# The row maxima of two cross-attentions, scheduled 1.4 units ahead of their scores instead of 2

## The chip, the core and the metric

The kernel runs on one core of a Trainium2 chip. The metric is the device time of one execution in microseconds (us). Engines: PE is TensorE (matrix products; PEld is its weight load), DVE is VectorE, ACT is ScalarE, POOL is GpSimd, SP is SyncE, which here only issues DMAs.

## The reference

A decoder of four layers works on `x`, 8 sequences of 256 tokens and 128 features, with a context of 1601 tokens and 64 features. Each layer adds a cross-attention to the context and then a feed-forward block. Attentions 0 and 3, which the change touches, have 16 heads of 8 features. Cut to what matters, for attention 0:

```
qh = (q @ Wq + bq).reshape(B, LQ, HEADS, D_K).transpose(0, 2, 1, 3)
kh = (k @ Wk + bk).reshape(B, LKV, HEADS, D_K).transpose(0, 2, 1, 3)
vh = (v @ Wv + bv).reshape(B, LKV, HEADS, D_K).transpose(0, 2, 1, 3)
scores = jnp.einsum('bhqd,bhkd->bhqk', qh, kh) * scale
attn = jax.nn.softmax(scores, axis=-1)
out = jnp.einsum('bhqk,bhkd->bhqd', attn, vh)
return concat @ Wo + bo
...
x = x + _L0_xattn_ref(_layernorm(x, axis=-1), ctx_512, ctx_512, ...)
```

The softmax needs, for each query and head, a number near the largest score, so that the exponential stays in range. Computing these maxima is the work that is moved here.

## The kernel before, in words

The function `narrow` does attention 0 at the start of the kernel and attention 3 near its end, each for the 8 sequences. The work of a sequence `b` is cut into four units of four heads, so an attention has 32 units, `n = 4 b + i`.

For a unit, `place` (lines 783 to 794) spreads keys and queries over the partitions with DMAs: 8 for the keys (on SP's queue) and 10 for the queries (on POOL's), into one of four places of a ring `K[n % 4]`, `Q[n % 4]`. A row of `Q`, zero at first, later holds minus the maximum, so that the score matmul itself subtracts it. Each place has two halves, `t` = 0 and 1, and each half holds two heads, one in partitions 0 to 63 and one in 64 to 127. Two matmuls on the two partition halves (`g` = 0, 1) can run side by side in the array.

Three pieces of work belong to a unit:

- *Maxima* (`maxima`, lines 796 to 823): 14 pairs and a shift. A pair is two matmuls into two buffers of the PSUM pool `pm` (line 807) and two DVE reduces (line 810) that take their row maxima. Twelve of the pairs have 512 columns in a matmul; the other two take the 66 columns left over, with four small matmuls each. `pm` has three buffers. The shift (lines 816 to 819) is three small DVE instructions that join the maxima and split them into two summands in `M`.
- *Placing the shift* (`place_shift`, lines 825 to 832): PE transposes `M` (line 828), ACT copies the result (line 830), and SP issues two DMAs that write the rows into `Q` (line 832).
- *Scores and values*: a unit has 7 steps `p` of two half steps `t`. A half step computes the scores of two chunks of 128 context tokens (`score`: line 994 on PE into buffers of pool `st`, of which there are four; line 997, two exponentials on ACT), then one chunk of values of the step before (`values`, line 1006 on PE). The first half step of a unit has the last chunk of the unit before, the second has none.

The order on each engine is the order in which the program writes the instructions; no scheduler changes it. In each half step of unit `n` the loop at the end of `narrow` writes: the scores, a chunk of values, then what is in the list `beside` and has come due (placing keys and queries for unit `n + 3`, placing the shift, projections of queries, keys and values for the next sequence, loads), then the maxima that are due. Each entry of `beside` has a share of the unit at which it is due.

The maxima of unit `n + 2` are spread over the 14 half steps of unit `n`. Unit 0 has two sets, those of units 1 and 2, and units 30 and 31 have none; unit 0's own maxima are done ahead of the loop. The shift of unit `n + 1` is placed at share 0.1 of unit `n`, which is half step 1; in unit 0 it is placed at the end.

In the last six units of attention 0 (from `AFTER = 26`), steps of the following feed-forward block for the first sequence stand in `beside` too.

The code that the diff touches, with the profile's line numbers:

Of the kernel before, what the change touches and what calls it, by code (L numbers as in the profile page):

```python
# [49 lines left out]
TAKEN = -3.0e38  # L50
KW = LK + 1
RING = 4
AFTER = 26


@with_exitstack
def decoder_kernel(ctx: ExitStack, tc: tile.TileContext, a: dict, out: bass.AP):
# [93 lines left out]
    for b in range(NB):  # L151
        x = const.tile([P, QT, D], F32, tag=f"x{b}", name=f"x{b}")
# [470 lines left out]
    def narrow(wq, wkT, wvT, wo, bq, bk, bv, bo, first, after=None):  # L623
# [8 lines left out]
        with ExitStack() as es:  # L632
# [163 lines left out]
            def maxima(n):  # L796

                mx = two.tile([P, QT, 4, 4], F32, tag="mx", name="mx", bufs=3)
                last = KW - 1536

                def pair(t, js, at, w):
                    k, q = K[n % RING][t], Q[n % RING][t]
                    pt = [pm() for g in range(2)]
                    for x, j in enumerate(js):
                        for g in range(2):
                            r = slice(64 * g, 64 * g + 64)
                            nc.tensor.matmul(pt[g][:, x * w:(x + 1) * w], lhsT=q[r, j * P:(j + 1) * P],  # L807
                                             rhs=k[r, at:at + w], start=True, stop=True)
                    for g in range(2):
                        nc.vector.tensor_reduce(mx[:, js[0]:js[-1] + 1, 2 * t + g, at // 512],  # L810
                                                pt[g][:, 0:len(js) * w].rearrange("p (j k) -> p j k", k=w),
                                                AX.X, ALU.max)

                def shift():
                    m = two.tile([P, QT, 4], F32, tag="mxn", name="mxn")
                    nc.vector.tensor_reduce(m, mx, AX.X, ALU.max, negate=True)
                    mq = M[n % 2].rearrange("p j (h s) -> p j h s", s=8)
                    nc.vector.tensor_copy(mq[:, :, :, 0], m)
                    nc.vector.tensor_tensor(mq[:, :, :, 1], m, mq[:, :, :, 0].bitcast(F32), ALU.subtract)

                return [f for t in range(2) for f in
                        (*(lambda j=j, t=t, at=at: pair(t, (j,), at, 512) for j in range(QT) for at in (0, 512, 1024)),
                         lambda t=t: pair(t, range(QT), 1536, last))], shift

            def place_shift(n):
                pt = bank()
                for j in range(QT):
                    nc.tensor.transpose(pt[0:32, j * P:(j + 1) * P], M[n % 2][:, j, :].bitcast(F32), ident)
                st = two.tile([32, LQ], F32, tag="st32", name="st32")
                nc.scalar.copy(st, pt[0:32, 0:LQ])  # L830
                for t in range(2):
                    nc.sync.dma_start(out=Q[n % RING][t][4:P:8, :].bitcast(F32), in_=st[16 * t:16 * t + 16, :])

# [100 lines left out]

            before = []
            steps = (NC + 1) // 2
            more = maxima(1)
            for n in range(units):
                b, i = divmod(n, 4)
                v = V[b % 2]  # L940

                ms = []
                if n == 0:
                    ms += [*more[0], more[1]]
                if n + 2 < units:
                    pairs, shift = maxima(n + 2)
                    ms += [*pairs, shift]
                due = [len(ms) * (x + 1) // (2 * steps) for x in range(2 * steps)]
                done = 0

                beside = []
                if n + 3 < units:
                    beside += [((0.0, 0.25)[t], lambda t=t: place(n + 3, t)) for t in range(2)]
                beside.append((0.3, lambda: load_later(3)))
                if n + 1 < units:
                    beside.append((1.0 if n == 0 else 0.1, lambda: place_shift(n + 1)))
                if b + 1 < NB and i == 0:
                    beside += zip((0.0, 0.2, 0.5, 0.65, 0.8, 1.0),
                                  (lambda: turn_y(b + 1), lambda: make_q(b + 1), *make_k(b + 1)))
                if b + 1 < NB and i == 1:  # L960
                    beside += zip((0.2, 0.4, 0.6, 0.8), make_v(b + 1))
                if b and i == 2:
                    beside += zip((0.2, 0.35, 0.6), finish(b - 1))
                if b + 2 < NB and i == 2:
                    load_ct(b + 2)
                    if first:
                        cuts, turns = make_ct(b + 2)
                        beside += zip((0.0, 0.0, 0.4, 0.6), cuts)
                        beside += zip((0.3, 0.5, 0.7, 0.9), turns)
                if b + 3 < NB and i == 3:  # L970
                    beside.append((0.0, lambda: load_raw(b + 3)))
                if b + 2 < NB and i == 3:
                    beside.append((0.5, lambda: (make_y(b + 2), add_bias(b + 2))))
                if after is not None and n >= AFTER:
                    if n == AFTER:
                        late = after(Scratch(), bank)
                    per = 2 * steps
                    beside += [((x - per * (n - AFTER)) / per, lambda x=x: run([late[x]], EARLY + LATE))
                               for x in late if x // per == n - AFTER]
                beside.sort(key=lambda x: x[0])  # L980
                if i == 0:
                    od[b] = two.tile([P, LQ], F32, tag="od", name="od")
                    sums[b] = two.tile([P, LQ], F32, tag="sums", name="sums")
                cell = {}

                def score(p, t, e):
                    k, q = K[n % RING][t], Q[n % RING][t]
                    cs = range(2 * p, min(2 * p + 2, NC))
                    m = P if cs[-1] < NC - 1 else LAST
                    st = [bank().rearrange("p (j q) -> p j q", q=LQ) for g in range(2)]  # L990
                    for j, c in enumerate(cs):
                        for g in range(2):
                            r = slice(64 * g, 64 * g + 64)
                            nc.tensor.matmul(st[g][0:m, j, :], lhsT=k[r, c * P:c * P + m], rhs=q[r, :],  # L994
                                             start=True, stop=True)
                    for g in range(2):
                        nc.scalar.activation(e[0:m, 2 * t + g, 0:len(cs), :], st[g][0:m, 0:len(cs), :], AF.Exp)  # L997

                def values(c, e, cell=cell, i=i, v=v, b=b):
                    if c == 0:  # L1000
                        cell["o"] = ps["o"].tile([P, LQ], F32, tag="o", name="ov")
                    m = P if c < NC - 1 else LAST
                    for g in range(4):
                        h = 4 * i + g
                        at = 2 * D * c + 32 * (h // 2) + 2 * (h % 2)
                        nc.tensor.matmul(cell["o"][32 * g:32 * g + 32, :], lhsT=v[0:m, at:at + 32],  # L1006
                                         rhs=e[0:m, g, c % 2, :], start=(c == 0), stop=(c == NC - 1))
                    if c == NC - 1:
                        os = two.tile([P, LQ], F32, tag="os", name="os")
                        nc.scalar.copy(os, cell["o"])  # L1010
                        at = slice(32 * i, 32 * i + 32)
                        nc.sync.dma_start(out=od[b][at, :], in_=os[0:P:4, :])
                        nc.sync.dma_start(out=sums[b][at, :], in_=os[1:P:4, :])

                for p in range(steps):
                    e = two.tile([P, 4, 2, LQ], F32, tag="e", name="e")
                    for t in range(2):
                        score(p, t, e)
                        if before:
                            before.pop(0)()  # L1020
                        while beside and (beside[0][0] * 2 * steps < 2 * p + t + 1 or p * t == steps - 1):
                            beside.pop(0)[1]()
                        for f in ms[done:due[2 * p + t]]:
                            f()
                        done = due[2 * p + t]
                    before = [lambda c=c, e=e, values=values: values(c, e)
                              for c in range(2 * p, min(2 * p + 2, NC))]
            for f in before + finish(NB - 1):
# [726 lines left out]
```

## Time and profile before

| what | value |
|---|---|
| median of 3 runs | 3657.8 us (3653.39 to 3658.94) |
| profiled execution, its own time | 3657.44 us |
| its span on the core | 3655.7 us |
| mean granted clock of TensorE | 0.968 |
| attention 0, first exponential to last copy of values | 65.8 to 743.9 us |
| attention 3, likewise | 2766.7 to 3418.2 us |

Times in the profile count from the start of the span. "Busy" is the time in which an engine works on at least one instruction; PE's matmuls overlap, and their ends are modelled, so a start is more certain than an end. A group of instructions gives the line, the engine, the tile written and those read, the size and the number; behind the bar stand busy time, the mean of one in ns, the idle time just before, and what ended it. In the timeline, equal instructions in a row are merged ("x4"), and idle time in brackets is followed by what ended it. In a table of stretches, a line is the stretch, its length, the busy time of PE, PEld, DVE, ACT and POOL with the number of instructions, the granted clock of TensorE (1.00 is full), the busy share of the DMA engines and what they moved in GB/s.

### The profile page before, as it was taken

The numbers are of one execution on the slowest core, as the hardware profiler recorded it, in microseconds if no ns is written. First come the engines' busy times: TensorE is split into PE (matmuls) and PEld (weight loads), VectorE is DVE, ScalarE is ACT, GpSimd is POOL, SyncE is SP. The second block draws the span as 40 slices with busy tenths as digits, with TensorE's granted clock in tenths as the row PEclk, the third lists the DMA queues.
The fourth block names the chain that finished last, engine by engine and source line by source line (L and its number), as shares of the span: only waits on it lengthen the run. The fifth ranks groups of instructions, "written<-read, shape, count | busy, mean of one in ns | idle before, by whom it ended". The sixth has DMA issues, their size and how long they took to land.

```text
span 3655.7 us, 74821 instructions
## 1 busy us (share of the span) xinstructions
PE 3437.5 (94%) x28363; PEld 2319.6 (63%) x28363; DVE 2600.6 (71%) x6564; ACT 2284.9 (63%) x5686; POOL 1126.8 (31%) x1993
## 2 busy tenths in 40 slices
PE   6999999979999999999999999988989999999799
PEld 3555555458777877787887878865434555555344
DVE  5788888656777766777777777675556888888365
ACT  2688888746566666666666666653223878888422
POOL 4344344614051513324150602020113333332100
PEclk9999999989999999999999999998985999999899
DMA  4354444230000001000000000020003444443100
GB/s 92 56 88 72 70 69 64 28 80 1 15 2 27 6 24 38 1 26 1 15 1 15 1 11 6 11 68 19 0 18 56 68 69 66 64 67 50 44 3 9
DMA packets 112118, 130.21 MB, mean 36 GB/s; under 512 B 67184, under 2 KB 95888, under 8 KB 111120
## 3 DMA queue, kind: packets, MB, share of 16 engines
q1 hardware_dynamic: 91024, 114.09, 18.3%
q0 software_dynamic: 20480, 10.53, 1.2%
q8 instruction: 225, 3.69, 0.4%
q10 hardware_dynamic: 256, 0.82, 0.2%
q14 instruction: 133, 1.09, 0.1%
HBM read 44.79 MB, written 11.28 MB: 15 GB/s over the span
## 4 chain that ended last, share of the span: by engine, by line
PE 79%; DVE 10%; ACT 6%; issue 2%; POOL 2%; DMA 1%; SPq 0%; ACTq 0%; DVEq 0%; POOLq 0%
PE ov L1006 13%; PE o L467 11%; PE st L420 11%; PE pm L807 10%; PE t L453 8%; PE st L994 6%; PE gu L1601 3%; PE gu L1602 3%; DVE mx L810 3%; PE o L1616 3%; ACT pt L455 2%; DVE ls L427 2%; PE st L778 2%; ACT e L441 1%; PE st L721 1%
## 5 line engine op out<-in xcount | busy, mean ns | idle before, releaser
L810 DVE TENSOR_REDUCE mx<-pm 128x1 f32<-128x512 f32 (+1 forms) x1792 | 1015.0, 626 | 221.6 <-PE pm L807 220.1
L997 ACT ACTIVATE e<-st 128x512 f32<-128x512 f32 (+1 forms) x1792 | 916.5, 564 | 250.0 <-PE st L994 193.2
L427 DVE TENSOR_REDUCE ls<-st 128x1 f32<-128x512 f32 x1088 | 548.7, 566 | 319.7 <-PE st L420 318.2
L441 ACT ACTIVATE e<-st,ls 128x512 f32<-128x512 f32 x1088 | 634.0, 602 | 12.8 <-DVE ls L430 12.0
L455 ACT COPY pt<-t 128x512 f32<-128x512 f32 x544 | 293.5, 586 | 460.4 <-PE t L453 459.7
L1006 PE MATMUL ov<-e,V 128*32 128x256 f32 x6656 | 556.1, 401 | 0.3 <-ACT e L997 0.3
L807 PE MATMUL pm<-K,Q 64*128 64x512 f32 (+1 forms) x2048 | 528.0, 468 | 26.9 <-DVE mx L810 19.4
L453 PE MATMUL t<-ident,e 128*128 128x128 f32 (+1 forms) x3536 | 507.1, 282 | 2.2
L467 PE MATMUL o<-pt,v 128*64 128x128 f32 (+1 forms) x7072 | 495.2, 280 | 11.9 <-DVE pt L455 7.9
L807 PEld LDWEIGHTS pm<-K,Q 64*128 64x128 f32 x2048 | 238.4, 195 | 374.6 <-DVE mx L810 261.2
L467 PEld LDWEIGHTS o<-pt,v 128*64 128x64 f32 (+1 forms) x7072 | 417.5, 139 | 83.0 <-issue 31.6
L453 PEld LDWEIGHTS t<-ident,e 128*128 128x128 f32 (+1 forms) x3536 | 392.4, 141 | 51.6 <-ACT pt L455 28.8
L994 PE MATMUL st<-Q,K 64*128 64x256 f32 (+1 forms) x3328 | 422.8, 296 | 0.3 <-ACT e L997 0.2
L420 PE MATMUL st<-ct,qh 128*128 128x512 f32 x1088 | 404.8, 372 | 2.3 <-ACT e L441 2.3
L994 PEld LDWEIGHTS st<-Q,K 64*128 64x128 f32 (+1 forms) x3328 | 343.8, 188 | 42.3 <-issue 14.6
L420 PE MATMUL st<-ct,ql 128*128 128x512 f32 x1088 | 361.8, 365 | 0.0
L793 POOL DMA_DIRECT2D Q<-qh x256 | 127.9, 500 | 469.3 <-PE st L994 415.9
L455 DVE COPY pt<-t 128x512 f32<-128x512 f32 (+1 forms) x544 | 239.1, 481 | 35.3 <-PE t L453 35.1
L420 PEld LDWEIGHTS st<-ct,qh 128*128 128x128 f32 x1088 | 204.7, 188 | 86.8 <-issue 38.4
L1604 ACT ACTIVATE act<-gu 128x512 f32<-128x512 f32 x132 | 78.8, 597 | 250.3 <-PE gu L1602 248.1
L441 ACT ACTIVATION_READ_ACCUMULATOR e<-st,ls 128x1 f32 x1088 | 230.7, 212 | 0.0
L420 PEld LDWEIGHTS st<-ct,ql 128*128 128x128 f32 x1088 | 205.5, 189 | 36.8
(444 smaller groups left out, 4205.5 us busy)
## 6 DMA issues: line engine op xcount, KB each, us to landing
K<-kh SPq DMA_DIRECT2D x252, 100.1 KB
K<-kl SPq DMA_DIRECT2D x252, 100.1 KB
ct<-ctd SPq DMA_DIRECT2D x24, 801.0 KB
ctd<-ct SPq DMA_DIRECT2D x8, 801.0 KB
v<-in_ctx SPq DMA_DIRECT2D x16, 384.0 KB
Q<-qh POOLq DMA_DIRECT2D x256, 16.0 KB, 2.5
Q<-ql POOLq DMA_DIRECT2D x256, 16.0 KB, 2.5
raw<-in_ctx SPq DMA_DIRECT2D x8, 384.0 KB
```

The source lines that it names most:

```text
L420: nc.tensor.matmul(st[n, c][:, 0:w], lhsT=q[k, h][i][:, j * P:(j + 1) * P], rhs=ct[k][:, at:at + w], start=(i == 0), stop=(i == 1))
L427: nc.vector.tensor_reduce(ls[n][:, c:c + 1], st[n, c][:, 0:BANK[c][1]], AX.X, ALU.max)
L441: nc.scalar.activation(e[n][:, at:at + w], st[n, c][:, 0:w], AF.Exp, bias=ls[n][:, 4:5], scale=1.0, accum_out=ls[n][:, 5 + c:6 + c])
L453: nc.tensor.transpose(t[0:m, (c - 4 * i) * P:(c - 4 * i + 1) * P], e[n][:, c * P:c * P + m], ident)
L455: (nc.scalar.copy if i < 2 else nc.vector.tensor_copy)(p[0:m, 0:w], t[0:m, 0:w])
L467: nc.tensor.matmul(o[n][half, 0:P], lhsT=v[k][0:m, c, :], rhs=turned[n, c // 4][0:m, (c % 4) * P:(c % 4 + 1) * P], start=(c < 2), stop=(c ...
L793: nc.gpsimd.dma_start(out=q[r:P:8, :].bitcast(F32), in_=qhl[b][r % 2][src, :].bitcast(F32))
L807: nc.tensor.matmul(pt[g][:, x * w:(x + 1) * w], lhsT=q[r, j * P:(j + 1) * P], rhs=k[r, at:at + w], start=True, stop=True)
L810: nc.vector.tensor_reduce(mx[:, js[0]:js[-1] + 1, 2 * t + g, at // 512], pt[g][:, 0:len(js) * w].rearrange("p (j k) -> p j k", k=w), AX.X, ...
L994: nc.tensor.matmul(st[g][0:m, j, :], lhsT=k[r, c * P:c * P + m], rhs=q[r, :], start=True, stop=True)
L997: nc.scalar.activation(e[0:m, 2 * t + g, 0:len(cs), :], st[g][0:m, 0:len(cs), :], AF.Exp)
L1006: nc.tensor.matmul(cell["o"][32 * g:32 * g + 32, :], lhsT=v[0:m, at:at + 32], rhs=e[0:m, g, c % 2, :], start=(c == 0), stop=(c == NC - 1))
```

## The change

The maxima are no longer tied to a unit's own list. A function `plan(m)` gives each of the 15 tasks of unit `m` (14 pairs, then the shift) a half step counted from the start of the attention, from half step 8 of unit `m - 2` up to half step 8 of unit `m - 1`, with the task's place rounded down; for unit 1 they start at 0. The loop then takes the tasks of each half step. The shift of unit `n + 1` is placed at share 9/14 of unit `n`. In the new kernel the lines behind the edit are three or four further down.

```diff
+DONE = 8
...
             steps = (NC + 1) // 2
-            more = maxima(1)
+            per = 2 * steps
+            tasks = {}
+
+            def plan(m):
+
+                pairs, shift = maxima(m)
+                first_, last_ = max(0, per * (m - 2) + DONE), per * (m - 1) + DONE
+                todo = [*pairs, shift]
+                for x, f in enumerate(todo):
+                    tasks.setdefault(first_ + (last_ - first_) * x // len(todo), []).append(f)
+
+            plan(1)
             for n in range(units):
                 b, i = divmod(n, 4)
                 v = V[b % 2]
-
-                ms = []
-                if n == 0:
-                    ms += [*more[0], more[1]]
                 if n + 2 < units:
-                    pairs, shift = maxima(n + 2)
-                    ms += [*pairs, shift]
-                due = [len(ms) * (x + 1) // (2 * steps) for x in range(2 * steps)]
-                done = 0
+                    plan(n + 2)
...
                 if n + 1 < units:
-                    beside.append((1.0 if n == 0 else 0.1, lambda: place_shift(n + 1)))
+                    beside.append(((DONE + 1) / per, lambda: place_shift(n + 1)))
...
-                        for f in ms[done:due[2 * p + t]]:
+                        for f in tasks.pop(per * n + 2 * p + t, []):
                             f()
-                        done = due[2 * p + t]
```

More of the change, by code (lines that the diff above doesn't have):

```diff
@@ L976, in narrow @@
                         late = after(Scratch(), bank)
-                    per = 2 * steps
                     beside += [((x - per * (n - AFTER)) / per, lambda x=x: run([late[x]], EARLY + LATE))
```

## The prediction

> **What bounds the kernel now.** I read the page first, then busy time in stretches cut at the units of the two attentions, then the PE timeline inside one unit, then the order of instructions of both kernels on each engine.
>
> ```profile
> PE 3437.5 (94%) x28363; PEld 2319.6 (63%) x28363; DVE 2600.6 (71%) x6564; ACT 2284.9 (63%) x5686; POOL 1126.8 (31%) x1993
> PE 79%; DVE 10%; ACT 6%; issue 2%; POOL 2%; DMA 1%; SPq 0%; ACTq 0%; DVEq 0%; POOLq 0%
> L810 DVE TENSOR_REDUCE mx<-pm 128x1 f32<-128x512 f32 (+1 forms) x1792 | 1015.0, 626 | 221.6 <-PE pm L807 220.1
> ```
>
> PE is busy 94% and is 79% of the chain. So I ask of each part of the change what it does to PE's own time, and where PE waits. By unit (attention 3: units 0, 1, 29, 30):
>
> ```profile
> 2764.70:2819.20 54.50, 49.83 (x227) 23.91 (x226) 31.78 (x58) 19.25 (x38) 11.32 (x19) 0.50 0.15 34
> 2819.20:2844.60 25.40, 25.40 (x218) 14.61 (x218) 16.36 (x32) 16.86 (x34) 4.01 (x9) 0.78 0.40 61
> 3368.30:3385.70 17.40, 17.40 (x193) 9.28 (x192) 16.30 (x32) 14.65 (x30) 0.00 (x0) 1.00 0.02 7
> 3385.70:3401.90 16.20, 15.98 (x168) 7.58 (x167) 3.50 (x9) 14.20 (x30) 0.91 (x2) 1.00 0.03 9
> ```
>
> [...]Unit 29 is filled by PE; DVE (16.3) and ACT (14.7) fit inside. Unit 30 has no maxima and is only 1.2 us shorter, since ACT then sets the pace. Unit 0 takes 54.5 us at a clock of 0.50. Attention 0's unit 0 is the same (54.5); its clock column reads 1.00, but its value matmuls last 633 ns, as at 0.50, against 403 ns later, so I go by durations.
>
> In cold unit 0 each half step has two pairs, four maxima matmuls on three pm buffers:
>
> ```profile
> 2780.25 1.22 PE L807 MATMUL pm<-K,Q 64*128 64x512 f32 x3
> 2781.83 0.79 PE L807 MATMUL pm<-K,Q 64*128 64x512 f32 x1 [0.36 <-DVE mx L810]
> 2781.83 1.21 PE L994 MATMUL st<-Q,K 64*128 64x256 f32 x4
> 2782.97 1.08 PE L1006 MATMUL ov<-e,V 128*32 128x256 f32 x8
> 2783.98 1.22 PE L807 MATMUL pm<-K,Q 64*128 64x512 f32 x3
> ```
>
> The fourth waits for the first's reduce: it starts 1.58 us after the first, and the scores behind it take 1.14 us to the values instead of 0.56, because the two row halves no longer run side by side. A half step is 3.73 us. A cold half step with one pair (unit 1) is 2.16.
>
> Warm, in unit 29:
>
> ```profile
> 3369.35 0.50 PE L807 MATMUL pm<-K,Q 64*128 64x512 f32 x2
> 3369.68 0.40 PE L994 MATMUL st<-Q,K 64*128 64x256 f32 x4
> 3370.01 0.39 PE L828 MATMUL st<-ident,M 128*32 128x128 f32 x2
> 3370.34 0.79 PE L807 MATMUL pm<-K,Q 64*128 64x512 f32 x2
> 3370.67 0.68 PE L994 MATMUL st<-Q,K 64*128 64x256 f32 x4
> 3371.28 0.64 PE L1006 MATMUL ov<-e,V 128*32 128x256 f32 x8
> 3371.85 0.51 PE L807 MATMUL pm<-K,Q 64*128 64x512 f32 x2
> ```
>
> A pair alone: maxima 0.33, scores 0.33, values 0.57, together 1.24 to 1.28 a half step. Half step 1 has no values, so its second maxima matmul comes early. It starts 0.29 after the first (0.79 where 0.50 is usual), which is 1.28 us after 3369.35: a pm buffer comes back only 1.28 us after it was taken (0.53 until the reduce starts, 0.69 reduce, 0.05 wake-up). That wait hides the transposes of line 828. The figure is 1.27 to 1.29 in nearly all undisturbed units.
>
> **Part 1: unit 0 loses seven pairs.** The order shows half steps 0 to 6 of unit 0 unchanged, half step 7 with the shift alone, 8 with two pairs, 9 to 13 with one. Seven pairs leave (28 before, 21 after); the other units keep 14, unit 30 gets the seven. Half steps 7 to 13 take 29.7 us in both attentions (starts of line 994). After, still cold: 7: 0.56 + 1.01 + 1.15 (K projection) = 2.72; 8: 0.56 + 1.01 + 1.57 = 3.14; 9: 1.14 + 1.01 + 0.26 (transposes) + 1.15 + 0.59 = 4.15; 10: 2.16; 11: 3.31; 12: 1.95; 13: 2.3. Sum 19.7, a gain of 10.0 each.
>
> Then the clock. It rises after a stretch of PE work without waits: in attention 3 from 2818.7 to 2830.9 (12 us), in attention 0 from 117.7 to at most 125.2 (6 to 7), at the end of attention 0 from 680.6 to 690 (9 to 10). I take 8. After, such a stretch starts at half step 9, with 13.9 us of cold work ahead in unit 0: 5.9 of it turns warm, saving 43% (1.24 against 2.16), 2.5 us. Unit 1's cold start goes too: 5.3 us of it in attention 0, 11.4 in attention 3, saving 2.3 and 4.9. Together (10.0 + 2.5) x 2 + 7.2 = 32 us. The Trainium skill ("TensorE: Matmul & The Clock Gate", Part 1 on the clock gate) says some 3.4 us of sustained work warm it; the rows show two to three times that. By the page the gain would be 36. I stay with the rows; 26 to 38 as bounds.
>
> **Part 2: every later unit gets a double step.** 15 tasks over 14 half steps, rounded down: tasks 0 and 1 both fall in half step 8, and the shift alone in 7. Before, each half step had exactly one pair, and the shift rode on the last. The order shows the four 512-column matmuls in a row once per unit, 29 warm units (1 to 29) in each attention. No such wait stands there before; nearest rows are the cold double step and the 1.28 us of half step 1, which agree. Half step 7 becomes 0.34 shorter. In 8, scores and values 0.90, then 1.28 to the fourth matmul (DVE has been idle, so nothing shortens it): 2.18 where 1.24 was. In 9, scores to values take 0.61 (3370.67 to 3371.28) where 0.33 was. Sum: -0.34 + 0.94 + 0.28 = +0.88. Behind the wait on PE stand scores, thus ACT's exponentials, but ACT has 2.7 us of slack per unit; PE has none to catch up with. Bounds 0 (all absorbed) and 1.2; I take 0.87.
>
> **Part 3: the shift rows move** from half step 1 to 9: two transposes (PE), one copy of 0.35 us (ACT), two DMA issues of 0.9 us (SP). At 1 the transposes lay under the 1.28 us wait, so taking them away frees nothing; at 9 the pm buffers have been freed (second reduce ends 1.82 us after the first matmul, needed at 2.5), so 0.32 us is bare (3370.01 to 3370.34). Bounds 0 and 0.35; I take 0.31. ACT's copy falls in slack. On SP the two issues now stand behind both halves of the next K placement and weight loads, all issued and nearly all moved 12 us into a unit; half step 9 is about there, and the rows are needed five half steps, over 6 us, later, against some 4 us for copy, issue and transfer. Cost nothing; if that cover went, 1 to 2 us a unit. The shift's own DVE work (0.7 us) moves from the unit's end to an idle spot, worth nothing where the 1.28 us rule already ruled. But in attention 0 the transposes at half step 1 do wait for it (0.27 us in six units; 0.75, 0.74 and 1.20 in units 26, 28, 30): about -4 us in all.
>
> **Part 4: unit 30.** Seven pairs more in an ACT-paced unit: half steps 0 to 6 go from 8.0 to 8.8 us (those of unit 29), +0.9 in attention 3; attention 0's share is in the -4. K placement, loads and POOL issues keep their places: 0, and K has more lead.
>
> **Sum.** 29 x 2 x (0.87 + 0.31) = +68.4; -32.2; +0.9; -4. Net +33 on the profiled execution's 3657.4 us, which is 0.4 below the median: 3691 us, 0.9% slower.
>
> **Rivals.** *Absorbed bunch (faster).* In steady state the second maxima matmul of many half steps starts 0.05 us after a reduce ends, so PE may really be paced by the buffer loop and could run ahead. Then half step 7 gives back what 8 costs, and only the transposes stay: 3657.4 - 35 + 18 = 3640 to 3645. It decides if the fourth matmul starts at most 0.57 us after the first. Against: it was 1.58 cold, the loop is 1.28, and reduces of 0.6 us cannot be shortened. 10%. *Half of it (no change):* a loss near 0.6 per unit balances the gain, 3657; 6%. *Clock stays cold in unit 0:* only the 20 us of part 1, 3703; 8%. *Clock falls at each double step.* In attention 0:
>
> ```profile
> 704.33 0.50 PE L994 MATMUL st<-Q,K 64*128 64x256 f32 x4
> 706.03 0.38 PE L828 MATMUL st<-ident,M 128*32 128x128 f32 x2 [1.20 <-DVE M L819]
> 706.33 0.50 PE L994 MATMUL st<-Q,K 64*128 64x256 f32 x4
> 706.77 0.64 PE L1006 MATMUL ov<-e,V 128*32 128x256 f32 x8
> 707.34 0.65 PE L994 MATMUL st<-Q,K 64*128 64x256 f32 x4
> 707.91 1.08 PE L1006 MATMUL ov<-e,V 128*32 128x256 f32 x8
> ```
>
> A wait of 1.20 us was followed by cold matmuls (1.08), one of 0.75 in unit 26 was not. Mine would show as 0.55: the third matmul starts 0.23 after the first and lasts 0.50, the fourth starts at 1.28. The same page (section on HAM oscillation) sets the danger at gaps over about 3.4 us; this trace puts it near 1, so the margin is 0.6 us and not 2.9. A fall costs 1.1 us (here) to 4.1 (after 680.6): over 58 units 3755 or more; 5%. That the change does not do what it says is excluded by the order of instructions.
>
> **How the numbers follow.** Main case 71%, 3691, own range 3672 to 3712: part 1 by 6 either way, part 2 and 3 by 0.2 a unit (12 us). Faster by over 0.2% 10%, within 0.2% (about what a measurement here can tell from no change) 6%, slower 84%. The range 3662 to 3718 takes in the colder clock and reaches toward the balance.
>
> **What would show it.** Right: unit 0 near 40 us with 403 ns values by its end; units 2 to 29 about 1.2 us longer; a row of three maxima matmuls, then one after a 0.5 us wait on line 810's reduce, at half step 8; waits of PE on DVE up by about 0.5 x 58. Wrong: units 2 to 29 as long as before (then it is faster), or 633 ns values inside them (then far slower).

## The result and the profile after

The changed kernel takes 3698.4 us (median of 4 runs, 3696.16 to 3702.51) beside 3655.6 before (4 runs, 3650.64 to 3658.94): a ratio of 1.0121 [1.0106, 1.0136], or 42.8 us slower. Its profiled execution took 3697.88 us, with a span of 3696.2 against 3655.7.

On the page, the work is the same and the path hardly changes its shape. The line of busy times, the chain by engine, and the group of the reduces:

```profile
PE 3437.7 (93%) x28363; PEld 2311.2 (63%) x28363; DVE 2595.2 (70%) x6564; ACT 2286.2 (62%) x5686; POOL 1125.8 (30%) x1993
PE 78%; DVE 11%; ACT 6%; issue 2%; POOL 2%; DMA 1%; SPq 1%; ACTq 0%; DVEq 0%; POOLq 0%
L811 DVE TENSOR_REDUCE mx<-pm 128x1 f32<-128x512 f32 (+1 forms) x1792 | 1011.9, 627 | 266.4 <-PE pm L808 265.0
```

PE's busy time is the same to 0.2 us (3437.5 before), although one part of the span became faster and another slower. What has grown is DVE's share of the chain (10% before) and its idle time ahead of the reduces (221.6 before). So the stages have to be read, and first the waits. Of each line of PE's waits, the columns are the total in us, how often, and the longest. Before:

```profile
PE pm L807 <- DVE mx L810: 19.4, 51, 2.3
```

After:

```profile
PE pm L808 <- DVE mx L811: 64.4, 160, 0.7
```

That is 45 us more waiting for a maxima buffer. 58 waits of 0.55 in the double half steps make 32 of it. In half step 1, where the transposes used to fill the buffer wait, 0.32 of it is now bare in every unit, 19 us in all; this costs no time (half step 1 of unit 29 takes 0.95 now and took 0.99 before). Unit 0 and unit 28 of attention 0 have some 6 us of waits less.

The stretches that answer to those of before are unit 0 (attention 0, then attention 3), and units 1, 29 and 30 of attention 3:

```profile
63.70:104.70 41.00, 38.24 (x211) 18.54 (x210) 23.83 (x43) 19.26 (x39) 14.04 (x19) 0.58 0.31 59
2779.40:2818.70 39.30, 36.71 (x211) 18.13 (x210) 23.76 (x43) 18.85 (x38) 9.64 (x15) 0.61 0.21 47
2818.70:2841.00 22.30, 21.44 (x219) 12.41 (x218) 16.18 (x32) 16.95 (x35) 5.34 (x12) 1.00 0.45 65
3404.50:3423.50 19.00, 18.12 (x194) 9.37 (x194) 16.32 (x32) 14.75 (x30) 0.00 (x0) 1.00 0.02 6
3423.50:3442.00 18.50, 17.69 (x184) 8.69 (x183) 11.09 (x23) 14.29 (x30) 0.91 (x2) 1.00 0.03 8
```

Unit 0 is 13 to 15 us shorter (54.5 before). Unit 1 runs at a clock of 1.00 instead of 0.78. But unit 29, which stands for units 1 to 29 of each attention, is 1.6 us longer with the same 16.3 us of DVE. PE's timeline in unit 29, half steps 7 to 9 (the columns are start and length), before:

```profile
3377.13 0.48 PE L994 MATMUL st<-Q,K 64*128 64x256 f32 x4
3377.54 0.64 PE L1006 MATMUL ov<-e,V 128*32 128x256 f32 x8
3378.11 0.50 PE L807 MATMUL pm<-K,Q 64*128 64x512 f32 x2
3378.45 0.40 PE L994 MATMUL st<-Q,K 64*128 64x256 f32 x4
3378.77 0.64 PE L1006 MATMUL ov<-e,V 128*32 128x256 f32 x8
3379.34 0.54 PE L807 MATMUL pm<-K,Q 64*128 64x512 f32 x2
3379.68 0.44 PE L994 MATMUL st<-Q,K 64*128 64x256 f32 x4
...
3380.96 0.39 PE L994 MATMUL st<-Q,K 64*128 64x256 f32 x4
```

After:

```profile
3413.34 0.48 PE L998 MATMUL st<-Q,K 64*128 64x256 f32 x4
3413.76 0.64 PE L1010 MATMUL ov<-e,V 128*32 128x256 f32 x8
3414.32 0.50 PE L998 MATMUL st<-Q,K 64*128 64x256 f32 x4
3414.75 0.86 PE L1010 MATMUL ov<-e,V 128*32 128x256 f32 x8
3415.55 0.73 PE L808 MATMUL pm<-K,Q 64*128 64x512 f32 x3
3416.83 0.50 PE L808 MATMUL pm<-K,Q 64*128 64x512 f32 x1 [0.56 <-DVE mx L811]
3416.84 0.73 PE L998 MATMUL st<-Q,K 64*128 64x256 f32 x4
3417.49 0.64 PE L1010 MATMUL ov<-e,V 128*32 128x256 f32 x8
3418.07 0.39 PE L829 MATMUL st<-ident,M 128*32 128x128 f32 x2
3418.39 0.50 PE L808 MATMUL pm<-K,Q 64*128 64x512 f32 x2
```

The whole cost in a unit is in these lines. Half step 7 (from 3413.34) has no maxima. Half step 8 (3414.32) has four, the last of which starts 1.28 us after the first; its scores then need 0.65 to the values behind them. Half step 9 has two bare transposes (3418.07 to 3418.39). From start to start of the scores, in us:

| unit 29, attention 3 | before | after | change | predicted |
|---|---|---|---|---|
| half step 7 | 1.32 | 0.98 | -0.34 | -0.34 |
| half step 8 | 1.23 | 2.51 | +1.28 | +0.94 |
| half step 9 | 1.28 | 1.89 | +0.61 | +0.59 |
| the others | | | 0 | 0 |

The account of the profiled executions, from starts of scores and in us:

| stage | change | predicted |
|---|---|---|
| unit 0, both attentions (-13.4, -15.2) | -28.6 | -25.0 |
| warm start of unit 1 (-2.0, -4.5) | -6.5 | -7.2 |
| units 1 to 29, double step, transposes, shift (without the line above) | +74.2 | +64.4 |
| unit 30 (attention 0 +0.6, attention 3 +2.4) | +2.9 | +0.9 |
| unit 31 and outside the two attentions | -1.5 | 0 |
| sum | +40.5 | +33 |

The value of +74.2 is the growth of units 1 to 29 as measured, +29.4 in attention 0 and +38.3 in attention 3, with the 6.5 of unit 1's clock put back. The units are not all alike: those with i = 3 grew by 1.54, i = 1 by 1.56, i = 0 by 1.14, and those with i = 2 by 1.59 in attention 3 but 1.00 in attention 0 (means of units 4 to 25).

### The profile page after: what moved, and what is told of

It reads as the page before. It is cut to its first block, busy times and chain, and to the rows that moved or that the text cites. A ratio compares the mean times of both kernels' runs of the same rounds, so it can differ in the third digit from the quotient of the medians.

```text
span 3696.2 us, 74679 instructions
## 1 busy us (share of the span) xinstructions
PE 3437.7 (93%) x28363; PEld 2311.2 (63%) x28363; DVE 2595.2 (70%) x6564; ACT 2286.2 (62%) x5686; POOL 1125.8 (30%) x1993
## 4 chain that ended last, share of the span: by engine, by line
PE 78%; DVE 11%; ACT 6%; issue 2%; POOL 2%; DMA 1%; SPq 1%; ACTq 0%; DVEq 0%; POOLq 0%
PE ov L1010 13%; PE o L468 11%; PE st L421 11%; PE pm L808 10%; PE t L454 8%; PE st L998 6%; DVE mx L811 4%; PE gu L1604 3%; PE gu L1605 3%; PE o L1619 3%; ACT pt L456 2%; DVE ls L428 2%; PE st L779 2%; ACT e L442 1%; PE st L722 1%
## 5 line engine op out<-in xcount | busy, mean ns | idle before, releaser
L808 PE MATMUL pm<-K,Q 64*128 64x512 f32 (+1 forms) x2048 | 535.8, 453 | 71.9 <-DVE mx L811 64.4
L468 PEld LDWEIGHTS o<-pt,v 128*64 128x64 f32 (+1 forms) x7072 | 417.7, 139 | 82.8 <-issue 31.9
L998 PE MATMUL st<-Q,K 64*128 64x256 f32 (+1 forms) x3328 | 440.4, 297 | 0.1
L998 PEld LDWEIGHTS st<-Q,K 64*128 64x128 f32 (+1 forms) x3328 | 336.0, 185 | 57.5 <-issue 25.7
L1010 PEld LDWEIGHTS ov<-e,V 128*32 128x32 f32 x6656 | 142.1, 108 | 140.8 <-issue 40.6
```

What stands on the lines that cost most here:

```text
L468: nc.tensor.matmul(o[n][half, 0:P], lhsT=v[k][0:m, c, :], rhs=turned[n, c // 4][0:m, (c % 4) * P:(c % 4 + 1) * P], start=(c < 2), stop=(c ...
```

## The experiments

The theory was the prediction's: the double half step at 8 costs about 1.2 us a unit (more, as measured), and the bare transposes at 9 another 0.33. The rival was that the shorter lead itself costs time: keys, queries, shift rows or maxima late, a new wait in every unit. Of the 0.34 by which the double step came out dearer than predicted, two explanations stood: A, an exponential of half step 7 is late for the values of 8, since 7 had become shorter; B, semaphore waits on PE's queue ahead of a unit's first maxima. In each experiment the edit is against the changed kernel, unless it says otherwise.

**e1_even**: the same lead, one pair in each of the 14 half steps, the shift beside the last.

```diff
-                    tasks.setdefault(first_ + (last_ - first_) * x // len(todo), []).append(f)
+                    tasks.setdefault(first_ + (last_ - first_) * min(x, 13) // 14, []).append(f)
```

> The changed kernel with the tasks spread so that each half step of a warm unit has exactly one pair and the shift rides on the last pair (half step 7); the lead and the place of the transposes (half step 9) stay. Theory: the loss is the double half step, so units 2 to 29 come back from +1.55 us each to about +0.3 (the bare transposes), and unit 0 keeps its gain (35 us in both attentions with unit 1): 3655.6 - 35 + 19 + 3 - 4 = about 3639 us. Rival, the shorter lead itself costs (late rows of the shift, placement of keys and queries): units stay over 1.2 us longer and the time near 3690 us.

Measured: 3617.6 us (3611.44 to 3622.18), ratio to before 0.9897 [0.9881, 0.9913]. That is 80.7 us below the changed kernel and 36 below the kernel before. PE in unit 29, from half step 8:

```profile
3332.40 0.50 PE L998 MATMUL st<-Q,K 64*128 64x256 f32 x4
3332.83 0.64 PE L1010 MATMUL ov<-e,V 128*32 128x256 f32 x8
3333.40 0.50 PE L808 MATMUL pm<-K,Q 64*128 64x512 f32 x2
3333.73 0.40 PE L998 MATMUL st<-Q,K 64*128 64x256 f32 x4
3334.06 0.64 PE L1010 MATMUL ov<-e,V 128*32 128x256 f32 x8
3334.63 0.40 PE L829 MATMUL st<-ident,M 128*32 128x128 f32 x2
```

No wait is left; only the transposes (0.33) are still bare. Units with i = 3 and i = 1 are 0.3 us above the kernel before, which is the transposes; those with i = 0 are equal to it, those with i = 2 below. Unit 0 is 38.2 and 38.3. So the lead of 1.4 units is innocent, and the rounding that put two pairs into one half step is the cost. The lists of waits say the same: neither here nor in the changed kernel does a score wait for a DMA.

The 3639 expected was missed by 21. Of the profiled gain, about 13 us lie outside the attentions (2309.3 against 2322.1), which no edit here touches; such differences between executions are why stages are compared inside the attentions. Most of the rest is that units with i = 0 and i = 2 do not pay the 0.3. In units 26 and 28 of attention 0, PE waits 0.91 and 2.43 us for a reduce, and value matmuls of 633 ns follow, so this kernel has time left there too.

**e2_done9**: the place of the double step moved by one half step, `DONE = 9`. Half step 8 is now the empty one, and the double step is the odd one, 9.

> The changed kernel with DONE = 9: the empty half step is 8 and the double one 9, the transposes are in half step 10. Of the 1.55 us a unit, 0.34 more stands in the double half step than I worked out. Theory A: values of an even half step read what the exponentials of the odd one before have just written, so a shortened half step 7 only runs into a wait in 8; with an even half step empty the 0.34 is given back: 58 x 0.34 = 20 us less, and 3 us less in unit 0: about 3676 us. Theory B: PE's sequencer takes four waits for the placing DMAs at the first pair of a unit, 0.1 us each, wherever that pair stands: about 3695 us.

Measured: 3673.7 us (3664.45 to 3687.44), ratio 1.0064 [1.004, 1.0089]. The double step in unit 29:

```profile
3383.04 0.50 PE L998 MATMUL st<-Q,K 64*128 64x256 f32 x4
3383.48 0.64 PE L1010 MATMUL ov<-e,V 128*32 128x256 f32 x8
3384.05 0.73 PE L808 MATMUL pm<-K,Q 64*128 64x512 f32 x3
3385.33 0.49 PE L808 MATMUL pm<-K,Q 64*128 64x512 f32 x1 [0.55 <-DVE mx L811]
3385.33 0.73 PE L998 MATMUL st<-Q,K 64*128 64x256 f32 x4
```

The step takes 2.29 us instead of 2.51. The difference is in the values: 0.64 here, with 0.57 until the maxima start, against 0.86 and 0.80 in the changed kernel. An even half step takes values of a new step `p`; in the changed kernel an exponential they need ended at 3414.94. Three of the eight value matmuls started at 3414.75, four from 3414.99 on and the last at 3415.24, where e2 has four and four. So A holds for 0.23 of the 0.34. B falls: if a semaphore wait in front of the first maxima cost anything here, it would stand between values and maxima, and 0.57 is the usual figure. The other 0.10 stand between scores and values: 0.44 here and 0.43 in the changed kernel, 0.33 in the sum. That is what scores cost that do not follow a pair of 512 columns, and the kernel before showed it, in the lines of its unit 29 above. Scores to values are 0.41 behind the small maxima of 66 columns (3377.13), and 0.32 behind the pair (3378.45). Why is not shown by any run.

The changed kernel confirms A a second time, in its units with i = 0. There two matmuls of the next keys' projection stand in half step 7, which lasts 1.65 us and leaves the exponentials time; half step 8 takes 2.29, as in e2.

Units 1 to 29 are 11 us shorter in all than in the changed kernel, where A had expected 20; units with i = 0 lost 0.12 each, and in unit 26 of attention 0 the clock fell. More, over 17 us, lies in unit 0, 31.0 and 31.9 us, because the clock rose early: the changed kernel's unit 0 has a clock of 0.58 to 0.61, while in e2 the values of attention 3 turn from 1.08 us in half step 2 to 0.64 in half step 4:

```profile
2768.96 1.08 PE L1010 MATMUL ov<-e,V 128*32 128x256 f32 x8
...
2774.95 0.64 PE L1010 MATMUL ov<-e,V 128*32 128x256 f32 x8
...
2776.79 0.50 PE L808 MATMUL pm<-K,Q 64*128 64x512 f32 x1 [0.55 <-DVE mx L811]
...
2777.46 0.64 PE L1010 MATMUL ov<-e,V 128*32 128x256 f32 x8
```

With `DONE = 9` half step 2 has one pair of unit 1 instead of two, and PE had no wait for some 7 us. The waits of 0.55 behind it did not take the clock away.

**e3_between**: the transposes put between the two pairs of the double step, where PE waits anyway.

```diff
-                    beside.append(((DONE + 1) / per, lambda: place_shift(n + 1)))
+                    tasks.setdefault(per * n + DONE, []).insert(1, lambda n=n: place_shift(n + 1))
```

> The changed kernel with the two transposes (and the copy and DMAs behind them) moved from half step 9 to half step 8, between its two pairs. Theory: PE waits there for a pm buffer, 1.28 us after the first matmul, whatever it does in between, so the transposes are hidden: 58 x 0.33 = 19 us less, about 3679 us. Rival: PE is not really idle there, or the transposes push the fourth matmul out: no change, 3698 us.

Measured: 3684.2 us (3677.26 to 3686.86), ratio 1.0077 [1.0061, 1.0094], 14.2 below the changed kernel. Half step 8 of unit 29 from its maxima on, and the scores of 9:

```profile
3400.00 0.50 PE L808 MATMUL pm<-K,Q 64*128 64x512 f32 x2
3400.43 0.40 PE L829 MATMUL st<-ident,M 128*32 128x128 f32 x2
3400.76 1.02 PE L808 MATMUL pm<-K,Q 64*128 64x512 f32 x2
3401.28 0.72 PE L998 MATMUL st<-Q,K 64*128 64x256 f32 x4
```

The fourth maxima matmul still starts 1.28 us after the first (3400.00; the scores behind it start at 3401.28), the transposes lie inside, and half step 9 is 0.33 shorter. That confirms the step of the transposes; 58 x 0.33 would be 19, but units with i = 0 gain only 0.14.

**e4_even10**: e1 with `DONE = 10`, so that the shift is placed at half step 11, three ahead of its use.

> The even spread with DONE = 10: maxima end at half step 9 of the unit before, transposes in half step 11, three half steps (3.8 us) before the rows are needed. Unit 0 has 18 pairs where DONE = 8 leaves 21, worth 5 us cold in each attention. Theory: copy, issue and transfer of the rows take about 4 us, so PE waits 0 to 0.5 us a unit: 3630 to 3655 us. Rival, the rows take much longer (queues of SP and DMA): over 1 us a unit, 3690 us or more.

Measured: 3616.6 us (3605.85 to 3620.56), ratio 0.9891 [0.9871, 0.9911], as e1; later units as e1, unit 0 32.8 and 32.9. That is below the 3630 to 3655 expected. With three half steps left the rows are just late in places, as this line of its waits shows (scores that wait for the DMA of the rows):

```profile
PE st L998 <- DMA Q<-st: 2.8, 6, 0.6
```

No such line stands in the lists of the changed kernel and of e1, where five half steps are left. So the rival's wait exists, but not at the lead of the change, and here it costs 3 us and not 1 us a unit.

**e5_after_m4 and e6_before_m4**: the size of the PSUM pools, four buffers for maxima and three for scores instead of three and four, in the changed kernel (e5) and in the kernel before (e6, the control).

```diff
-            es.enter_context(psum(m=3, s=4, o=1))
+            es.enter_context(psum(m=4, s=3, o=1))
```

> The changed kernel with four pm buffers and three st buffers instead of three and four. Theory, the fourth maxima matmul of the double half step waits for a buffer: with a fourth buffer that wait (0.55 us shown, 1.2 us of a unit with what follows) is gone, and the double half step is short; what three st buffers cost shows in its control beside it. Time of this one minus the control: 43 - 70 = about -27 us (-10 to -40). Rival, the wait is another (readiness of K and Q, PE's own sequencer): the difference stays near +43 us.

> Control for the run beside it: the kernel before with four pm and three st buffers. The wait in half step 1 (1.28 us from first to second matmul) shrinks, but scores then wait for the exponentials; either may win: 3640 to 3760 us. What counts is the difference between the two.

Measured: e5 3606.3 us (two runs, 3604.85 and 3607.81), ratio 0.9863 [0.9844, 0.9883]; e6 3624.8 (two runs, 3624.72 and 3624.94), ratio 0.9914 [0.9894, 0.9934], which is less than the 3640 to 3760 expected. With a fourth buffer the change makes the kernel 18.5 us faster, where with three it made it 42.8 slower. The double half step in e5:

```profile
2892.04 0.67 PE L1010 MATMUL ov<-e,V 128*32 128x256 f32 x8
2892.64 0.73 PE L808 MATMUL pm<-K,Q 64*128 64x512 f32 x4
2893.21 0.39 PE L998 MATMUL st<-Q,K 64*128 64x256 f32 x4
```

The four maxima matmuls start within 0.57 us and the step takes 1.78. By unit, those with i = 3 are 0.19 us longer in e5 than in e6, and those with i = 1 0.21, where the change cost them 1.54 and 1.56 with three buffers. The price is in e5's list of waits, scores that wait for a buffer from the exponentials:

```profile
PE st L998 <- ACT e L1001: 22.3, 61, 1.0
```

So the double step costs what it does because of the 1.28 us round trip of three buffers.

**e7_even9 and e8_ramp9**: even spread with `DONE = 9` (e7); and in e8 also, for unit 1's maxima alone, one pair in half steps 0 to 3 and two in 4 to 8, to have no waits at the start and to be done early.

> The even spread with DONE = 9. With DONE = 9 half step 2 of unit 0 has one pair, so PE has nearly 7 us without a wait from half step 1 on, and in the run with DONE = 9 and the rounding of the change the clock then rose at half step 2 to 3 and stayed up through later waits of 0.55 to 0.75 us. Theory, a stretch without waits warms the clock, and waits that short do not cool it again: unit 0 is about 30 us in both attentions where the even spread with 8 has 38, so about 16 us less than that one: 3602 us. Rival, that early warming was chance: unit 0 36 to 38 us, 3615 us.

> As the even spread with DONE = 9, but unit 1's maxima in unit 0 go one pair each in half steps 0 to 3 and two each in 4 to 8, so that PE has no wait for some 9 us at the start. Theory: the clock is up by half step 3 or 4, and the double half steps then take 2.4 us each (DVE's pace) and not 3.7: unit 0 29 to 31 us, 3602 us. Rival, the clock stays low as long as the maxima come in pairs: unit 0 36 us or more, 3615 us.

Measured: e7 3611.0 us (3609.0 to 3613.55), 0.9877 [0.9861, 0.9894]; e8 3610.5 (3608.42 to 3615.02), 0.9877 [0.9862, 0.9891]. The two are equal, and both missed their 3602. In e7 unit 0 is 29.4 and 30.0 as expected, but units with i = 0 are 0.3 longer than in e1, and the rest of the miss is open. In e8 unit 0 is 32.3 and 30.9: the clock was up by half step 3, and fell again in both attentions after a row of double steps, for half steps 9 and 10 in attention 0 (values of 633 ns, after waits of 0.36, 0.56 and 0.42 us) and for half step 9 in attention 3.

**e9_even_m4 and e10_even9_m4**: even spread and four buffers, with `DONE` 8 and 9.

> Even spread (DONE = 8) with four pm and three st buffers: the two remedies together. With four buffers the change still takes 1.00 + 1.78 us for half steps 7 and 8 where two single ones are 2.5, so the even spread should give back about 0.28 us x 58 = 16 us of 3606: 3590 us, plus or minus 8 for when the clock rises in unit 0. Rival, both remedies remove the same wait and nothing is left to win: 3604 us or more.

> The same with DONE = 9, whose unit 0 had the clock up by half step 3 to 4 in both attentions: 3588 us if that holds with four pm buffers, 3600 us or more if the double half steps of unit 0 keep the clock low here.

Measured: e9 3592.7 us (3591.5 to 3595.84), 0.9837 [0.9822, 0.9853]; e10 3593.2 (3592.13 to 3597.0), 0.9841 [0.9821, 0.986]. These beat both kernels, by 59 us against the one before. e9 came as expected; e10 missed its 3588, and in attention 0 its clock did not rise by half step 4 (values of 633 ns until 78.0). Their order between themselves is open.

## Why the prediction was right, and where a term was off

The sign and the mechanism were right; the total was 7.5 us low on the profiled execution (+33 against +40.5). That it came so near is in part luck, since errors pulled against each other: some 21 us too little for the double step (58 x 0.36, from the units with i = 3) and 2 for unit 30, against 6 too much for the units with i = 0 (14 x 0.41), and gains put too small by 7 in the late units and the i = 2 units of attention 0 and by 3 in unit 0.

*Part 1, unit 0 and the start of unit 1 (-32.2 predicted, -35.1 measured).* The seven pairs left as worked out. The clock rose sooner than at "8 us from half step 9". In attention 0 the last wait ended at 94.2 and the first 403 ns values came at 100.5, 6.3 us later. In attention 3 it rose ahead of half step 9, after 6.2 us without a wait (2804.0 to 2810.2): the fourth maxima matmul of the double step is the first warm one.

```profile
2808.01 1.08 PE L1010 MATMUL ov<-e,V 128*32 128x256 f32 x8
2809.02 1.14 PE L808 MATMUL pm<-K,Q 64*128 64x512 f32 x3
2810.60 0.49 PE L808 MATMUL pm<-K,Q 64*128 64x512 f32 x1 [0.44 <-DVE mx L811]
...
2811.26 0.64 PE L1010 MATMUL ov<-e,V 128*32 128x256 f32 x8
```

The total landed near the 36 that the 3.4 us of the Trainium skill (the section that the prediction names) would have given, but not for that reason: both stretches here were over 6 us. The range that the prediction took from the kernel before was also too narrow: after the wait that ended at 706.03 in attention 0, values were warm again at 711.22, 5.2 us later.

*Part 2, the double step (+0.87 a unit predicted, +1.22 in unit 29).* The 1.28 us to the fourth matmul, the wait of 0.56 and the slower scores of half step 9 (0.32 for 0.28) came as worked out; e1 and e5 show that the double step and the buffers make the cost. The term that failed is half step 8's "scores and values 0.90": it measured 1.23. Of the 0.33, 0.10 is that scores behind an empty half step take 0.43 to the values and not 0.33, and 0.23 is the late exponential. "Half step 7 becomes 0.34 shorter" was true on PE and could not be kept, because ACT does not follow a half step as fast as PE then goes: its two exponentials take 0.59 each, and PE's half step 0.98. The sentence "ACT has 2.7 us of slack per unit" is a mean over the unit; within two half steps there was none. 58 x 0.35 is 20 us.

*Part 3, transposes and shift (+0.31 a unit, -4 predicted).* The transposes are bare by 0.32 to 0.33, and e3 takes them away again. In units with i = 0 they are bare by less: behind them stands a keys' projection (line 722), which starts 0.15 us after the first transpose, where maxima start 0.32 after. That and the half step 8 of 2.29 make the 1.14 of these units, which a sum taken from i = 3 does not give.

Attention 0 lies about 11 us below what its units would cost at the rates of attention 3, and the prediction had 4. It misread two of its waits: the 0.75 in unit 26 is a maxima matmul that waits for a reduce, and the 0.74 in unit 28 is the transposes waiting for an exponential; only the six of 0.27 and the 1.20 waited for the shift. More than half of the 11, 6.3, stands in units 28 and 29, where a wait of 2.27 us at half step 12 (before, at 680.57) and the half clock behind it are gone; the prediction did not price them. What removed that wait is not shown: with the same lead e1 has it, 2.43 us long. The rest is in units 26 and 27 and those with i = 2.

The SP queue's cover held at the lead of the change; in e4, with two half steps less, six waits for the rows show its edge.

*Part 4, unit 30 (+0.9 predicted, +2.4 and +0.6 measured).* It was held against unit 29, where i = 1. Unit 30 has i = 2, and an i = 2 unit of the kernel before takes 10.2 us for half steps 0 to 6 (unit 14 of attention 3) and not 8.8; unit 30 now takes 10.2 as well. In attention 0 the 1.20 us wait that went away hides most of this.

*Rivals.* The absorbed bunch is refuted by its own mark, 1.28 us to the fourth matmul instead of 0.57 at most. The clock did not stay cold in unit 0, and no value matmul in units 2 to 29 is cold after the change, so one wait of 0.56 a unit does not bring the clock down here. The margin of 0.6 us is not shown: in e5 and e10 the clock fell after a single wait of 0.38 (last section).

## What to carry to other kernels

When n tasks are laid over n - 1 or n + 1 slots, look at what the rounding doubles and what it leaves empty: here one slot of two pairs and one of none cost about 1.2 us in most of 58 units, and the same lead without it was 1% faster than before. How many matmuls may stand in one slot is read from the buffer round trip (first matmul to the reduce's end, 1.28 us with three buffers), and a fourth buffer or one task a slot removes the wait. A gain in one step is kept only up to the next dependency, so price the step together with the one behind it.

## What the runs showed of the hardware

From PE's last wait of over 0.15 us to the first warm row (matmuls of full-clock length) the time in the first units was 7.8 and 11.8 us before, 6.3 and 6.2 after, 6.9 and 7.3 in e2, 9.1 twice in e1, and 12.8 and 13.7 in e3. The extremes lie in other runs: between 3.0 and 4.0 us in e8 (attention 3; the wait ended at 2764.04, maxima at 2767.02 were cold, values at 2768.05 warm), and over 16 in e10 (attention 0; the wait ended at 61.84, maxima at 78.56 were still cold). What sets it within that range is open. The Trainium skill ("TensorE: Matmul & The Clock Gate", Part 1 on the clock gate) has about 3.4 us, which fits the shortest of these and not the longer ones.

Once up, the clock stood waits of 0.55 to 0.75 us in the changed kernel and in e2. It fell after single waits of 1.20 and 2.27 before and 0.91 in e1, in e8 after the row of double steps, and in unit 31 of attention 3, which has no maxima, after one wait of 0.38 in e5 and e10. In e10 (the values behind it are cold, 1.08 where 0.64 is warm):

```profile
3338.13 0.51 PE L998 MATMUL st<-Q,K 64*128 64x256 f32 x3 [0.38 <-ACT e L1001]
...
3340.04 1.08 PE L1010 MATMUL ov<-e,V 128*32 128x256 f32 x8
```

So no length of wait separates the cases, and what else counts is open.
